# Mamba block with a Hadamard-rotated MLP: elementwise work moved from VectorE to GpSimd, inner channels split in PSUM, scan inputs made two groups ahead

## The chip, the cores and the metric

One Trainium2 chip; the program runs on one of its cores. The metric is the device time of one execution in microseconds, given as the median of three runs. The engines are called PE (TensorE; PEld is its weight load), DVE (VectorE), ACT (ScalarE), POOL (GpSimd) and SP (the queue that issues nearly all DMAs).

## The reference

The input is (4, 1024, 512) in float32, so 4096 tokens. `LN` has no gain and no bias.

```python
x = x + LN(mamba(LN(x)))
x = x + LN(ffn(LN(x)))

def mamba(h):                                   # 1024 inner channels, 16 states, conv of 4 taps
    hidden, gate = split(h @ W_in + b_in)
    u = silu(causal_depthwise_conv(hidden, conv_w, conv_b))
    dt, B, C = split(u @ W_x)                   # 128 + 16 + 16 columns
    delta = softplus(dt @ W_dt + b_dt)
    A = -exp(a_log)
    # over the tokens t, for each channel d and state n:
    #   h[d,n] = exp(delta[t,d] * A[d,n]) * h[d,n] + delta[t,d] * u[t,d] * B[t,n]
    #   y[t,d] = sum over n of h[d,n] * C[t,n]
    y = (y + u * d_param) * silu(gate)
    return y @ W_out + b_out

def ffn(z):                                     # 512 -> 2048 -> 512
    z = fwht(z * SU_ug) / 64                    # normalised Walsh-Hadamard transform
    a = silu(z @ W_gate.T * (ws_gate * 64)) * (z @ W_up.T * (ws_up * 64))
    a = fwht(a * SU_dp) / 64
    return a @ W_down.T * (ws_down * 64)
```

## The kernel before

The 4096 tokens go in 16 chunks `c` of 256 (`TC`), four chunks to a sequence. Channels lie on the partitions: `d` counts 8 blocks of 128 channels, `m` pairs of blocks, `g` groups of four states. A chunk has 8 x 4 = 32 scan groups, called slots, and everything else is hung on them: a plan (`STEADY`, and variants for the first, second and last chunk) says at which slot of which chunk each step is written down. While chunk `c` is scanned, the same 32 slots hold the out projection, both layernorms and the MLP's first half of chunk `c-1`, the MLP's second half of `c-2`, and the in projection, convolution, `x_proj`, delta and softplus of chunk `c+1`. This gives the order in which the program is written; the framework's planner then fixes the order on each engine from its own cost model. A queue works strictly in the order that it was given, and waits with all that stands behind.

One scan group (`scan`, L446) is: on DVE `h = du * b` (L461, 128x1024), where `du` is delta times u and sits in PSUM (L452, made once for a pair of blocks) and `b` is B spread over all partitions in SBUF; on ACT four exponentials into two PSUM buffers `da` (L469); on DVE two scans of 512 (L470), each of which waits for two of the exponentials; on POOL a copy of the last column to `state` (L472) and `h * c` (L473); where the plan's string `add` has a P, a POOL addition of the two halves of `h` (L478); and on PE 8 transposes of 128x128 (4 after an addition) that add up in the PSUM tile `yt` (L484). An exponential needs its `da` buffer back from the scan before last.

`h` has five buffers. The PSUM pool `mm` has four, one bank each, shared by all matmul outputs: `pp` (in projection), `pf` (MLP first half), `pq` (second half), `po` (out projection), `pd` (delta) and the transposes. The weight streams share five buffers (`ring`, L255).

The MLP's first half goes by 16 inner blocks `f`: 24 matmuls into `pf` (`inner`, L574), then `inner_act`: tanh on ACT (L588) and two DVE instructions (L589, L590) into `hf` in SBUF. `inner_parts` makes two float16 parts for a pair of blocks: ACT rounds `hf` to float16 (L595), POOL subtracts (L596). The matmuls of the second half (L608) take both parts.

`ln_stats` makes a layernorm's scale `rs` and offset `nm` for two 128-token tiles: DVE statistics (L200, L201), two to four tiny DVE instructions (L206 to L212), and a POOL power (L209). `add_normalised` adds the residual: ACT adds `nm` to x (L220), and DVE does `src * rs + x` (L221).

`softplus` (slots 30 and 31) is a chain ACT, DVE, ACT, DVE, POOL for the next chunk's delta, with a change of the activation table for the logarithm. `carry` takes the state over a chunk's border. `spread` loads one group's `b` and `c` (two DMAs of 512 KB on SP).

Of the kernel before, what the change touches and what calls it, by code (L numbers as in the profile page):

```python
# [114 lines left out]
def block_kernel(  # L115
# [77 lines left out]
    def ln_stats(src, name, scale=None):  # L193


        n = len(src)
        mv = sb.tile([P, NJ, 2], F32, tag="mv", name=f"mv_{name}", bufs=4)
        for i, t in enumerate(src):
            st = sb.tile([P, 6], F32, tag="st", name=f"st_{name}_{i}", bufs=4)
            nc.vector.bn_stats(st, t)  # L200
            nc.vector.bn_aggr(mv[:, i, :], st)  # L201
        rs = sb.tile([P, NJ], F32, tag="rs", name=f"rs_{name}", bufs=4)
        nm = sb.tile([P, NJ], F32, tag="nm", name=f"nm_{name}", bufs=4)
        v = rs[:, 0:n]
# [7 lines left out]
        nc.vector.scalar_tensor_tensor(nm[:, 0:n], mv[:, 0:n, 0], -1.0, v, ALU.mult, ALU.mult)  # L212
        return rs, nm
# [4 lines left out]
    def add_normalised(dst, src, rs, nm, j, x):  # L218

        nc.scalar.activation(x, x, AF.Identity, bias=nm[:, j : j + 1])  # L220
        nc.vector.scalar_tensor_tensor(dst, src, rs[:, j : j + 1], x, ALU.mult, ALU.add)  # L221

# [222 lines left out]

    def scan(c, d, g):  # L446
        first, last = c % NTC == 0, c % NTC == NTC - 1
        m, i = d // 2, d % 2
        dl = live["dl", c, d // 4][:, d % 4, :]
        if g == 0 and i == 0:  # L450
            du = ps_du.tile([P, 2, TC], F32, tag="du", name=f"du_{c}_{m}")
            nc.vector.tensor_tensor(  # L452
                du, live["dl", c, d // 4][:, d % 4 : d % 4 + 2, :], live["u", c, m], ALU.mult
            )
            live["du", c, m] = du
        ns = slice(g * GN, (g + 1) * GN)
        h = sb.tile([P, GN, TC], F32, tag="h", name=f"h_{c}_{d}_{g}", bufs=5)
# [3 lines left out]
        nc.vector.tensor_tensor(  # L461
            h[:, :, t:], live["du", c, m][:, i, t:].unsqueeze(1).to_broadcast([P, GN, TC - t]),
            live["b", c, g][:, :, t:], ALU.mult,
        )
# [6 lines left out]
        if not last:  # L471
            nc.gpsimd.tensor_copy(state[:, d, ns], h[:, :, TC - 1])  # L472
        nc.gpsimd.tensor_tensor(h, h, live["c", c, g], ALU.mult)  # L473
# [107 lines left out]
    def inner_act(c, f):  # L581

        if f == 0:
            live["hp", c] = fp.tile([P, NF, 2, TC], F16, tag="hp", name=f"hp_{c}", bufs=1)
        if f % 2 == 0:
            live["hf", c] = fp.tile([P, 2, TC], F32, tag="hf", name=f"hf_{c}_{f}", bufs=2)
# [3 lines left out]
        nc.vector.scalar_tensor_tensor(t, pp[:, 1, :], cf[:, f : f + 1], t, ALU.mult, ALU.mult)  # L590

    def inner_parts(c, f):
        hp, hf = live["hp", c], live.pop(("hf", c))
        at = slice(f - 1, f + 1)
        nc.scalar.copy(hp[:, at, 0, :], hf)  # L595
        nc.gpsimd.tensor_tensor(hp[:, at, 1, :], hf, hp[:, at, 0, :], ALU.subtract)  # L596

# [286 lines left out]
    for c in range(NCH):  # L884
# [215 lines left out]
```

## Time and profile before

| what | value |
|---|---|
| runs | 3088.71 us median (3088.61 to 3094.82) |
| the profiled execution | 3092.33 us, its span 3090.5 us |
| busy of the span | DVE 93%, PE 79%, POOL 68%, ACT 62%, PEld 60% |
| start, and first chunk | 0 to 51 us, 51 to 292 us |
| second chunk | 292 to 526 us |
| steady chunks from 884 to 2664 us (ten) | 178.0 us each |
| last chunk, and the end behind it | 2838 to 3026 us, 3026 to 3090 us |
| HBM read and written | 415.14 MB, 25.69 MB; DMA queue q1 43.1% |

A chunk is counted from its first scan. A group's row in the profile gives the line, engine, operation, tiles, shapes and count, then busy time and the mean length of one instruction, then the engine's idle time just before them and who ended it. Busy time is a union, so a group of overlapping instructions has less of it than count times mean.

### The profile page before, as it was taken

The numbers are of one execution on the slowest core, as the hardware profiler recorded it, in microseconds if no ns is written. First come the engines' busy times: TensorE is split into PE (matmuls) and PEld (weight loads), VectorE is DVE, ScalarE is ACT, GpSimd is POOL, SyncE is SP. The second block draws the span as 40 slices with busy tenths as digits, with TensorE's granted clock in tenths as the row PEclk, the third lists the DMA queues.
The fourth block names the chain that finished last, engine by engine and source line by source line (L and its number), as shares of the span: only waits on it lengthen the run. The fifth ranks groups of instructions, "written<-read, shape, count | busy, mean of one in ns | idle before, by whom it ended". The sixth has DMA issues, their size and how long they took to land.

```text
span 3090.5 us, 45909 instructions
## 1 busy us (share of the span) xinstructions
PE 2442.0 (79%) x16119; PEld 1846.4 (60%) x16119; DVE 2865.0 (93%) x3677; ACT 1924.5 (62%) x4321; POOL 2098.4 (68%) x1788
## 2 busy tenths in 40 slices
PE   4657578787897879788696978879777887868788
PEld 3446466574766657476574757566565756556556
DVE  7998998999999899999999999999999999899973
ACT  5657556576666757567575766667575666657542
POOL 2675666677776768667585877768676767768661
PEclk8778789899998989899898999989888999989999
DMA  5434246353353435334353534435343433535347
GB/s 209 177 103 144 72 126 199 110 158 135 117 184 124 151 123 166 102 127 168 109 185 116 166 121 136 159 110 171 132 155 117 151 136 110 177 102 173 122 153 249
DMA packets 154222, 443.82 MB, mean 144 GB/s; under 512 B 17928, under 2 KB 35208, under 8 KB 153992
## 3 DMA queue, kind: packets, MB, share of 16 engines
q1 hardware_dynamic: 153848, 440.83, 43.1%
q8 instruction: 127, 2.08, 0.3%
q14 instruction: 103, 0.84, 0.1%
q10 hardware_dynamic: 144, 0.07, 0.0%
HBM read 415.14 MB, written 25.69 MB: 143 GB/s over the span
## 4 chain that ended last, share of the span: by engine, by line
DVE 62%; PE 13%; issue 11%; POOL 7%; ACT 6%; DMA 1%; SPq 0%; DVEq 0%; POOLq 0%; ACTq 0%
DVE h L470 24%; DVE h L461 13%; DVE pp L313 4%; PE pf L574 4%; POOL h L473 3%; PE pq L608 3%; DVE du L452 2%; DVE hf L590 2%; PE pp L266 2%; PE yt L484 2%; DVE hf L589 2%; ACT da L469 1%; PE po L525 1%; DVE y L512 1%; POOL h L478 1%
## 5 line engine op out<-in xcount | busy, mean ns | idle before, releaser
L469 ACT ACTIVATE da<-dl,a_sb 128x255 f32<-128x255 f32 x2048 | 954.1, 474 | 765.3 <-DVE h L470 722.9
L473 POOL TENSOR_TENSOR h<-h,c 128x1024 f32<-128x1024 f32 x512 | 1228.1, 2402 | 175.5 <-DVE h L470 112.3
L470 DVE TENSOR_TENSOR_SCAN h<-da,h 128x512 f32<-128x512 f32 x1024 | 1216.2, 1205 | 25.2 <-ACT da L469 23.5
L574 PE MATMUL pf<-zT,wu 128*128 128x256 f16 x6144 | 756.8, 282 | 111.2 <-DVE hf L590 65.8
L574 PEld LDWEIGHTS <-wu 128*128 128x128 f16 x6144 | 620.0, 101 | 215.6 <-issue 118.6
L484 PE MATMUL yt<-ident,h 128*128 128x128 f32 x3180 | 476.5, 293 | 278.2 <-POOL h L473 96.3
L461 DVE TENSOR_TENSOR h<-du,b 128x1020 f32<-128x1020 f32 (+1 forms) x512 | 609.0, 1201 | 11.9 <-PE yt L484 11.0
L484 PEld LDWEIGHTS yt<-ident,h 128*128 128x128 f32 x3180 | 395.1, 151 | 352.1 <-POOL h L473 125.5
L472 POOL COPY state<-h 128x4 f32<-128x4 f32 x384 | 89.0, 232 | 512.9 <-DVE h L470 461.0
L608 PE MATMUL pq<-wd,hp 128*128 128x512 f16 x1536 | 368.3, 391 | 6.2 <-DVE o L543 4.3
L478 POOL TENSOR_TENSOR h<-h 128x512 f32<-128x512 f32 x226 | 300.2, 1329 | 4.6
L266 PE MATMUL pp<-xT,wh 128*128 128x256 f16 x1440 | 218.2, 322 | 56.2 <-DVE y L512 20.7
L608 PEld LDWEIGHTS <-hp 128*128 128x128 f16 x1536 | 154.4, 101 | 178.5 <-issue 32.0
L525 PE MATMUL po<-wo,y 128*128 128x512 f32 x512 | 231.4, 601 | 7.7 <-POOL y L515 5.2
L266 PEld LDWEIGHTS <-wh 128*128 128x128 f16 x1440 | 165.7, 116 | 105.4 <-issue 64.6
L266 PE MATMUL pp<-xT,wg 128*128 128x256 f16 x1536 | 189.9, 278 | 16.8 <-DVE zT L230 7.6
L596 POOL TENSOR_TENSOR hp<-hf,hp 128x512 f16<-128x512 f32 x128 | 158.5, 1239 | 62.6 <-ACT hp L595 62.2
L266 PEld LDWEIGHTS <-wg 128*128 128x128 f16 x1536 | 153.3, 100 | 49.2 <-issue 27.1
L313 DVE SCALAR_TENSOR_TENSOR pp<-pre,half,pp 128x256 f32<-128x256 f32 x384 | 179.0, 470 | 3.1 <-ACT pp L306 1.8
L588 ACT ACTIVATE hf<-pf,tf 128x256 f32<-128x256 f32 x256 | 119.5, 468 | 71.3 <-PE pf L574 70.9
L525 PEld LDWEIGHTS po<-wo,y 128*128 128x128 f32 x512 | 95.8, 193 | 113.3 <-issue 102.5
L589 DVE SCALAR_TENSOR_TENSOR hf<-hf,pf 128x256 f32<-128x256 f32 x256 | 103.1, 403 | 40.1 <-ACT hf L588 40.1
(195 smaller groups left out, 3039.6 us busy)
## 6 DMA issues: line engine op xcount, KB each, us to landing
wu<-ug SPq DMA_DIRECT2D x256, 512.0 KB, 3.4
wd<-dn SPq DMA_DIRECT2D x144, 512.0 KB, 3.6
b<-bcd SPq DMA_DIRECT2D x64, 512.0 KB, 4.1
c<-bcd SPq DMA_DIRECT2D x64, 512.0 KB, 5.4
wg<-win SPq DMA_DIRECT2D x64, 512.0 KB, 4.2
wo<-in_w_out_dram SPq DMA_DIRECT2D x64, 512.0 KB, 4.3
wh<-win SPq DMA_DIRECT2D x60, 512.0 KB, 3.9
x<-in_x_dram SPq DMA_DIRECT2D x32, 256.0 KB, 2.7
```

Source lines behind the costliest of these rows:

```text
L266: nc.tensor.matmul(pp[:, i, :], lhsT=wt[:, a, k, i * P : (i + 1) * P], rhs=xT[:, b, k, :], start=(n == 0), stop=(n == KD * len(PARTS) - 1),)
L313: nc.vector.scalar_tensor_tensor(pp[:, i, :], pre[:, i, k : k + TC], half[:, k * ND + d : k * ND + d + 1], pp[:, i, :], ALU.mult, ALU.add,)
L461: nc.vector.tensor_tensor(h[:, :, t:], live["du", c, m][:, i, t:].unsqueeze(1).to_broadcast([P, GN, TC - t]), live["b", c, g][:, :, t:], A ...
L469: exp = nc.scalar.activation(da[:, n, 1:], dl[:, 1:], AF.Exp, scale=a_sb[:, d, k : k + 1])
L470: add = nc.vector.tensor_tensor_scan(two, flat(da), two, 0.0, ALU.mult, ALU.add)
L473: nc.gpsimd.tensor_tensor(h, h, live["c", c, g], ALU.mult)
L478: (nc.gpsimd if by == "P" else nc.vector).tensor_tensor(h[:, 0:parts, :], h[:, 0:parts, :], h[:, parts:, :], ALU.add)
L484: nc.tensor.matmul(yt[:, j, :], lhsT=h[:, n, j * P : (j + 1) * P], rhs=ident, is_transpose=True, start=(g == 0 and n == 0 and j == 0), sto ...
L525: last = nc.tensor.matmul(live["po", c][j], lhsT=live["y", c, m][:, i, j * P : (j + 1) * P], rhs=wt[:, i, :], start=(m == 0 and i == 0), s ...
L574: nc.tensor.matmul(pp[:, w, :], lhsT=wt[:, w, k // 2, a, k % 2, :], rhs=zT[:, b, k, :], start=(n == 0), stop=(n == KD * len(PARTS) - 1),)
L589: nc.vector.scalar_tensor_tensor(t, t, 1.0, pp[:, 0, :], ALU.add, ALU.mult)
L608: nc.tensor.matmul(live["pq", c, j], lhsT=hp[:, 2 * q + i, b, j * P : (j + 1) * P], rhs=wt[:, :, i, a, :], start=(q == 0 and i == 0 and (a ...
```

## The change

GpSimd takes over `delta * u` (into SBUF, `dus`; ACT copies it to PSUM for the products that stay on DVE), ten of the 32 products `du * b` of a steady chunk (string `mul`; five in the second chunk, none in the first), the small layernorm instructions, and the residual sum, for which ACT now applies scale and offset in one instruction. In return ACT copies the `state` column, and the steady `add` string has ten P instead of sixteen. The inner channels' second DVE instruction writes into PSUM, ACT rounds from there to float16, PE subtracts the rounded part in PSUM with a matmul by -1, and ACT writes the rest as the second part, block by block. The input of a scan group is made two groups ahead (`prepare`, `AHEAD`), with seven `h` buffers. `x_proj`, delta and softplus come two to four slots earlier, `spread` two. The buffers of tag `pa`, which three setup steps used, are gone: these steps take `h` buffers.

```diff
+AHEAD = 2
 STEADY = dict(
-    x=(21, 23),
-    delta=(25, 26, 26, 27),
-    soft=(30, 31),
+    x=(19, 20),
+    delta=(22, 23, 23, 24),
+    soft=(27, 28),
-    add="-P---PP--PP--PP---P--PPP-PP-P-PP",
+    mul="--P--P--P--P--P--P--P--P--P--P--",
+    add="-P--P---P--P--P--P--P--P--P--P--",
 FIRST = STEADY | dict(
+    mul="-" * SLOTS,
-    delta=(23, 23, 24, 25),
-    soft=(30, 30),
+    x=(20, 21),
+    delta=(22, 23, 23, 24),
+    soft=(27, 28),
 SECOND = STEADY | dict(
+    mul="-----P-----P-----P-----P-----P--",
-    delta=(21, 26, 27, 28),
+    delta=(21, 22, 23, 24),
...
+    neg16 = cp.tile([P, P], F16, name="neg16")
+    nc.vector.tensor_scalar(neg16, ident, -1.0, None, ALU.mult)
...
         if scale is None:
-            nc.vector.tensor_scalar(v, mv[:, 0:n, 1], sc[:, INV_D2 : INV_D2 + 1], EPS, ALU.mult, ALU.add)
+            nc.gpsimd.tensor_scalar(v, mv[:, 0:n, 1], sc[:, INV_D2 : INV_D2 + 1], EPS, ALU.mult, ALU.add)
         else:
-            nc.vector.tensor_scalar(v, mv[:, 0:n, 1], EPS, scale ** -2, ALU.add, ALU.mult)
+            nc.gpsimd.tensor_scalar(v, mv[:, 0:n, 1], EPS, scale ** -2, ALU.add, ALU.mult)
         nc.gpsimd.tensor_tensor(v, v, mhalf[:, 0:n], ALU.pow)
         if scale is None:
-            nc.vector.tensor_scalar(v, v, sc[:, INV_D : INV_D + 1], None, ALU.mult)
-        nc.vector.scalar_tensor_tensor(nm[:, 0:n], mv[:, 0:n, 0], -1.0, v, ALU.mult, ALU.mult)
+            nc.gpsimd.tensor_tensor(v, v, sc[:, INV_D : INV_D + 1].to_broadcast([P, n]), ALU.mult)
+        nc.gpsimd.tensor_tensor(nm[:, 0:n], mv[:, 0:n, 0], v, ALU.mult)
+        nc.gpsimd.tensor_scalar(nm[:, 0:n], nm[:, 0:n], -1.0, 0.0, ALU.mult, ALU.add)
...
     def add_normalised(dst, src, rs, nm, j, x):
-        nc.scalar.activation(x, x, AF.Identity, bias=nm[:, j : j + 1])
-        nc.vector.scalar_tensor_tensor(dst, src, rs[:, j : j + 1], x, ALU.mult, ALU.add)
+        normalised(src, src, rs, nm, j)
+        nc.gpsimd.tensor_tensor(dst, src, x, ALU.add)
...
+    def inputs(c, m, eng=nc.gpsimd):
+        by = PLANS[c]["mul"][2 * NG * m : 2 * NG * (m + 1)]
+        dl = live["dl", c, m // 2][:, 2 * (m % 2) : 2 * (m % 2) + 2, :]
+        if "-" in by:
+            du = live["du", c, m] = ps_du.tile([P, 2, TC], F32, tag="du", name=f"du_{c}_{m}")
+        if c == 0:
+            nc.vector.tensor_tensor(du, dl, live["u", c, m], ALU.mult)
+            return
+        dus = live["dus", c, m] = sb.tile([P, 2, TC], F32, tag="dus", name=f"dus_{c}_{m}")
+        eng.tensor_tensor(dus, dl, live["u", c, m], ALU.mult)
+        if "-" in by:
+            nc.scalar.copy(du, dus)
+
+    def prepare(c, d, g):
+        first = c % NTC == 0
...
+        h = live["h", c, d, g] = sb.tile([P, GN, TC], F32, tag="h", name=f"h_{c}_{d}_{g}", bufs=7)
         t = 0 if first else 1
         if not first:
             nc.scalar.copy(h[:, :, 0], live["h_0", c, m][:, i, ns])
-        nc.vector.tensor_tensor(
-            h[:, :, t:], live["du", c, m][:, i, t:].unsqueeze(1).to_broadcast([P, GN, TC - t]),
+        pool = PLANS[c]["mul"][d * NG + g] == "P"
+        (nc.gpsimd if pool else nc.vector).tensor_tensor(
+            h[:, :, t:],
+            live["dus" if pool else "du", c, m][:, i, t:].unsqueeze(1).to_broadcast([P, GN, TC - t]),
             live["b", c, g][:, :, t:], ALU.mult,
         )
+
+    def scan(c, d, g):
...
         if not last:
-            nc.gpsimd.tensor_copy(state[:, d, ns], h[:, :, TC - 1])
+            nc.scalar.copy(state[:, d, ns], h[:, :, TC - 1])
...
     def inner_act(c, f):
-        pp, t = live.pop(("pf", c, f)), live["hf", c][:, f % 2, :]
+        pp, hp = live["pf", c, f], live["hp", c]
+        t = fp.tile([P, TC], F32, tag="hf", name=f"hf_{c}_{f}", bufs=3)
         nc.scalar.activation(t, pp[:, 0, :], AF.Tanh, scale=tf[:, f : f + 1])
         nc.vector.scalar_tensor_tensor(t, t, 1.0, pp[:, 0, :], ALU.add, ALU.mult)
-        nc.vector.scalar_tensor_tensor(t, pp[:, 1, :], cf[:, f : f + 1], t, ALU.mult, ALU.mult)
+        nc.vector.scalar_tensor_tensor(pp[:, 1, :], pp[:, 1, :], cf[:, f : f + 1], t, ALU.mult, ALU.mult)
+        nc.scalar.copy(hp[:, f, 0, :], pp[:, 1, :])
 
     def inner_parts(c, f):
-        hp, hf = live["hp", c], live.pop(("hf", c))
-        at = slice(f - 1, f + 1)
-        nc.scalar.copy(hp[:, at, 0, :], hf)
-        nc.gpsimd.tensor_tensor(hp[:, at, 1, :], hf, hp[:, at, 0, :], ALU.subtract)
+        pp, hp = live.pop(("pf", c, f)), live["hp", c]
+        nc.tensor.matmul(
+            pp[:, 1, :], lhsT=neg16, rhs=hp[:, f, 0, :], start=False, stop=True, skip_group_check=True
+        )
+        nc.scalar.copy(hp[:, f, 1, :], pp[:, 1, :])
...
-        t = pr.tile([P, 2 * D], F32, tag="pa", name=f"ntd_{i}")
+        t = sb.tile([P, 2 * D], F32, tag="h", name=f"ntd_{i}", bufs=7)
...
-        t = pr.tile([P, NF, DB], F32, tag="pa", name=f"da_{b}")
+        t = sb.tile([P, NF, DB], F32, tag="h", name=f"da_{b}", bufs=7)
         nc.sync.dma_start(t, w_down_t[b])
-        t1 = pr.tile([P, NF, DB], F32, tag="pa", name=f"db_{b}")
+        t1 = sb.tile([P, NF, DB], F32, tag="h", name=f"db_{b}", bufs=7)
...
-        if c % NTC != 0:
-            for m in range(1, NM):
-                at(c, 2 * NG * m - 5, carry, c, m)
+        for m in range(1, NM):
+            at(c, 2 * NG * m - 6, inputs, c, m)
+            if c % NTC != 0:
+                at(c, 2 * NG * m - 7, carry, c, m)
...
-            if b % NTC != 0:
-                at(c, SLOTS - 1, carry, b, 0)
+                if q == 0:
+                    at(c, when["soft"][0], inputs, b, 0)
+                    if b % NTC != 0:
+                        at(c, when["soft"][0], carry, b, 0)
             for g in range(NG):
-                at(c, SLOTS - NG + g, spread, b, g)
+                at(c, SLOTS - NG + g - AHEAD, spread, b, g)
...
     for s in range(NCH * SLOTS):
         if s == 2 * SLOTS:
             hold.close()
+        if s + AHEAD < NCH * SLOTS:
+            prepare((s + AHEAD) // SLOTS, (s + AHEAD) // NG % ND, (s + AHEAD) % NG)
         if s > 0:
             scan(s // SLOTS, s // NG % ND, s % NG)
```

More of the change, by code (lines that the diff above doesn't have):

```diff
@@ L444, in carry @@
         live["h_0", c, m] = h
-    def scan(c, d, g):
-        first, last = c % NTC == 0, c % NTC == NTC - 1
-        m, i = d // 2, d % 2
[L449 to L455, printed above, removed]
+    def inputs(c, m, eng=nc.gpsimd):
[12 more added lines that the diff above has]
+        first = c % NTC == 0
+        m, i = d // 2, d % 2
         ns = slice(g * GN, (g + 1) * GN)
-        h = sb.tile([P, GN, TC], F32, tag="h", name=f"h_{c}_{d}_{g}", bufs=5)
+        h = live["h", c, d, g] = sb.tile([P, GN, TC], F32, tag="h", name=f"h_{c}_{d}_{g}", bufs=7)
         t = 0 if first else 1
@@ L460, in scan @@
             nc.scalar.copy(h[:, :, 0], live["h_0", c, m][:, i, ns])
-        nc.vector.tensor_tensor(
-            h[:, :, t:], live["du", c, m][:, i, t:].unsqueeze(1).to_broadcast([P, GN, TC - t]),
+        pool = PLANS[c]["mul"][d * NG + g] == "P"
+        (nc.gpsimd if pool else nc.vector).tensor_tensor(
+            h[:, :, t:],
+            live["dus" if pool else "du", c, m][:, i, t:].unsqueeze(1).to_broadcast([P, GN, TC - t]),
             live["b", c, g][:, :, t:], ALU.mult,
         )
+    def scan(c, d, g):
+        last = c % NTC == NTC - 1
+        dl = live["dl", c, d // 4][:, d % 4, :]
+        ns = slice(g * GN, (g + 1) * GN)
+        h = live.pop(("h", c, d, g))
         for q in range(2):
@@ L584, in inner_act @@
             live["hp", c] = fp.tile([P, NF, 2, TC], F16, tag="hp", name=f"hp_{c}", bufs=1)
-        if f % 2 == 0:
-            live["hf", c] = fp.tile([P, 2, TC], F32, tag="hf", name=f"hf_{c}_{f}", bufs=2)
-        pp, t = live.pop(("pf", c, f)), live["hf", c][:, f % 2, :]
+        pp, hp = live["pf", c, f], live["hp", c]
+        t = fp.tile([P, TC], F32, tag="hf", name=f"hf_{c}_{f}", bufs=3)
         nc.scalar.activation(t, pp[:, 0, :], AF.Tanh, scale=tf[:, f : f + 1])
         nc.vector.scalar_tensor_tensor(t, t, 1.0, pp[:, 0, :], ALU.add, ALU.mult)
-        nc.vector.scalar_tensor_tensor(t, pp[:, 1, :], cf[:, f : f + 1], t, ALU.mult, ALU.mult)
+        nc.vector.scalar_tensor_tensor(pp[:, 1, :], pp[:, 1, :], cf[:, f : f + 1], t, ALU.mult, ALU.mult)
+        nc.scalar.copy(hp[:, f, 0, :], pp[:, 1, :])
     def inner_parts(c, f):
-        hp, hf = live["hp", c], live.pop(("hf", c))
-        at = slice(f - 1, f + 1)
-        nc.scalar.copy(hp[:, at, 0, :], hf)
-        nc.gpsimd.tensor_tensor(hp[:, at, 1, :], hf, hp[:, at, 0, :], ALU.subtract)
+        pp, hp = live.pop(("pf", c, f)), live["hp", c]
[3 more added lines that the diff above has]
+        nc.scalar.copy(hp[:, f, 1, :], pp[:, 1, :])
     def down(c, q, js=range(NJ)):
@@ L632, in block_kernel @@
     h_sb = pr.tile([P, P], F32, name="h_sb", bufs=1)
-    wf = [sb.tile([P, KD, 2 * P], F32, tag="h", name=f"wf_{m}", bufs=5) for m in range(NM)]
-    wf += [pr.tile([P, KD, 2 * P], F32, tag="pa", name=f"wf_{m}") for m in range(NM, 2 * NM - 1)]
+    wf = [sb.tile([P, KD, 2 * P], F32, tag="h", name=f"wf_{m}", bufs=7) for m in range(NM)]
+    wf += [sb.tile([P, KD, 2 * P], F32, tag="h", name=f"wf_{m}", bufs=7) for m in range(NM, 2 * NM - 1)]
     wf += [sb.tile([P, KD, 2 * P], F32, tag="ring", name=f"wf_{2 * NM - 1}", bufs=5)]
@@ L720, in block_kernel @@
         softplus(0, 0, 1, nc.vector)
+        inputs(0, 0)
+        for s in range(AHEAD):
+            prepare(0, 0, s)
         for ins in scan(0, 0, 0):
@@ L949, in block_kernel @@
                 at(c, i + 1, inner_act, b, f)
-                if f % 2 == 1:
-                    at(c, i + 1, inner_parts, b, f)
+                at(c, i + 1, inner_parts, b, f)
         if c > 1:
@@ L1025, in block_kernel @@
             inner_act(c, f - 1)
-            if f % 2 == 0:
-                inner_parts(c, f - 1)
+            inner_parts(c, f - 1)
     inner_act(c, NF - 1)
```

## The prediction

> **What bounds the kernel now.** I read the engine shares first, then the stretches between chunk borders (a chunk runs from its first scan to the next one's), then the groups of the ten steady chunks alone, then the waits. The first lines are the page's, the next the stretches: length, busy time of PE, PEld, DVE, ACT, POOL, the granted PE clock, DMA share, GB/s.
>
> ```profile
> span 3090.5 us, 45909 instructions
> PE 2442.0 (79%) x16119; PEld 1846.4 (60%) x16119; DVE 2865.0 (93%) x3677; ACT 1924.5 (62%) x4321; POOL 2098.4 (68%) x1788
> ```
>
> ```profile
> 292.00:526.00 234.00, 172.02 (x1064) 131.61 (x1063) 214.89 (x299) 136.05 (x305) 151.45 (x134) 0.85 0.41 128
> ...
> 884.00:2664.00 1780.00, 1450.52 (x9817) 1096.39 (x9816) 1700.56 (x2130) 1152.88 (x2608) 1278.55 (x1101) 0.91 0.42 140
> ...
> 3026.00:3090.00 64.00, 56.53 (x422) 40.99 (x419) 18.83 (x43) 13.03 (x24) 10.34 (x10) 0.98 0.66 227
> ```
>
> The middle line is ten steady chunks of 178.0 us. In each, DVE is busy 170.1 us and idle 7.9, PE 145.1 busy and 32.9 idle, POOL 127.9, ACT 115.3. DVE bounds it; the next engine is PE at 81%. The groups of that stretch, with the instructions that go, and those that show what they will cost elsewhere:
>
> ```profile
> L473 POOL TENSOR_TENSOR h<-h,c 128x1024 f32<-128x1024 f32 x320 | 766.2, 2398 | 96.5 <-DVE h L470 66.3 <-PE po L525 5.0 <-DVE nm_d L212 4.3
> L484 PE MATMUL yt<-ident,h 128*128 128x128 f32 x1920 | 285.2, 290 | 158.5 <-issue 49.8 <-POOL h L478 46.7 <-POOL h L473 46.3
> L461 DVE TENSOR_TENSOR h<-du,b 128x1020 f32<-128x1020 f32 x228 | 271.3, 1200 | 6.5 <-PE yt L484 6.1 <-POOL h L473 0.3
> L478 POOL TENSOR_TENSOR h<-h 128x512 f32<-128x512 f32 x160 | 212.1, 1327 | 3.3
> L596 POOL TENSOR_TENSOR hp<-hf,hp 128x512 f16<-128x512 f32 x81 | 100.7, 1243 | 17.3 <-ACT hp L595 17.0
> L452 DVE TENSOR_TENSOR du<-dl,u 128x512 f32<-128x512 f32 x40 | 56.6, 1414 | 16.0 <-POOL dl L421 15.9
> L472 POOL COPY state<-h 128x4 f32<-128x4 f32 x256 | 56.1, 219 | 316.0 <-DVE h L470 287.5 <-PE po L525 6.5 <-DVE nm_d L212 4.6
> L515 POOL TENSOR_TENSOR y<-y,g 128x512 f32<-128x512 f32 x40 | 50.9, 1273 | 12.9 <-DVE y L512 12.9
> L595 ACT CAST hp<-hf 128x512 f16<-128x512 f32 x81 | 49.7, 614 | 19.8 <-DVE hf L590 19.8
> L420 DVE SCALAR_TENSOR_TENSOR dl<-dl,sp_w 128x1024 f32<-128x1024 f32 x20 | 36.9, 1844 | 2.9 <-ACT sp_w L419 2.9
> L221 DVE SCALAR_TENSOR_TENSOR x<-o,rs_b,xr 128x512 f32<-128x512 f32 x20 | 28.9, 1472 | 0.0
> L221 DVE SCALAR_TENSOR_TENSOR e<-e,rs_d,x 128x512 f32<-128x512 f32 x20 | 25.9, 1328 | 2.1 <-ACT x L220 2.1
> ```
>
> The waits of the same stretch say who follows whom:
>
> ```profile
> ACT da L469 <- DVE h L470: 438.3, 358, 6.0
> POOL state L472 <- DVE h L470: 287.5, 153, 9.2
> ...
> PE pf L574 <- DVE hf L590: 43.9, 27, 4.9
> ```
>
> ACT and POOL stand still for DVE's scans; PE waits for POOL's products (the L484 row), so for DVE at second hand, and for PSUM buffers that DVE gives back. Little waits the other way.
>
> **The change, per steady chunk.**
>
> *DVE.* Ten products: a product adds about 1.06 us to DVE's busy time (319 in the stretch add 338.7 us to the union; mean length 1.20), so 10.6. du: 56.6 / 10 = 5.7. Residual: (28.9 + 25.9) / 10 = 5.5. Tiny layernorm instructions L206, L208, L211, L212: 3.4 + 16.8 + 10.3 + 24.3 = 54.8 / 10 = 5.5. Sum 27.3, DVE falls to 142.8.
>
> *The rule against it.* By the rows, one 128x1024 product costs 1.20 us on DVE and 2.40 on POOL (L473), and the Trainium skill says the same and draws the opposite conclusion: "GPSIMD Engine Reference", section Engine selection, wants elementwise work on VectorE, being about twice as fast. Counted as work, ten moved products cost 24.0 us for 10.6; counted by the engine that is full, they gain 10.6, since POOL has 50.1 us idle and DVE 7.9. The page's Key points add that GpSimd shares SBUF interfaces with VectorE, which clashes with VectorE instructions that have two SBUF inputs. Here rows split: L221, du and L420 have two and run at 1.33 to 1.84 us, while products and scans (one input in PSUM) keep to 1.2 us. If a fuller POOL slowed every DVE instruction, the gain would go; by the rows it can slow only what still has two, the four softplus instructions (the least L420 took is near 1.2 for this size), so I add 1 us. DVE: 144.
>
> *POOL.* Ten products 24.0; du 4 x 1.27 (L515, same size) = 5.1; residual sums 5.1; 13 tiny instructions, not seen on POOL in this form: between the state copy's 0.22 and the power's 0.70 (L209), I take 0.25, near the tiny additions of the carry (0.24 to 0.28), 3.3 (at most 9.1). Less six additions of 1.33 (8.0), L596 (10.1), L472 (5.6). POOL: 127.9 + 13.8 = 141.7.
>
> *PE.* Six additions fewer mean 24 more transposes at 285.2 / 1920 = 0.149: 3.6 (up to 7 unpipelined at 0.29). The 16 matmuls by -1: 0.125 pipelined (an L574 matmul) to 0.39 alone with its weight load; I take 0.2: 3.2. PE: 152. The granted clock rose with PE's load in the shown stretches (0.85, 0.91, 0.98), so this may shrink by some per cent; I don't count on it.
>
> *ACT.* 32 copies of 256 out of PSUM at 0.37 (L498) = 11.8; 24 state copies at 0.18 = 4.3; four du copies at 0.61 = 2.4; fuller residual +0.4; less L595, 5.0. ACT: 129. Two waits are new. The state copy waits for a group's second scan; if it stands before the next exponentials, each is late by up to one scan, 1.1 us, up to 27 us a chunk; I take 0, as the planner can put it behind them, and exponentials wait for that same engine anyway. And the matmul by -1 waits for ACT's copy, with PE's next work queued behind it, while its `pf` bank is held through two ACT copies and a place in PE's queue: 0 to some 5 us each. Covers are the 24 matmuls (about 3 us) of the next block and three other `mm` banks; I price it within PE's idle below.
>
> *What moves.* The border: in the softplus chain near 1580 us DVE had 6 of the chunk's 7.9 us of idle. With softplus three slots earlier and inputs two ahead, scans can go on over it; late next would be DVE's scan behind the logarithm's two table loads (1.28 us each) on ACT. I keep 7.9 us as DVE's loss. The eight `spread` DMAs (b lands in a median 4.1, c in 5.4 us) pass two slots of SP's queue: b's buffer is free earlier, c's isn't, so a c load may stop the queue for two slots, with weight streams behind. Five ring buffers cover it (PE's weight loads waited for `wu` DMAs 7.4 us in the whole run), so 0; without cover a late load is 4 us. `x_split`'s small DMAs and the delta matmuls move with slack on both sides.
>
> *Sum.* DVE alone would allow 144 + 7.9 = 152 us. But then PE (152) would be full, and it does not run full anywhere: its densest long stretch is the end, 56.5 of 64 us (88%). At 92% (its clock higher, waits for DVE gone) 152 us of work make 165; DVE is then 87%, POOL 86%, ACT 78% busy. So 178 to 165, times 14 chunks (thirteen steady ones and the last): -182. Second chunk: five products, du, residual and layernorm off DVE, about -20, of which I give back 10, since `dn_load` takes `h` buffers two at a time from the scan. First chunk: its wf and norm tiles also take `h` buffers, +8. End: 16 matmuls by -1 and longer chains in the MLP, +3. Together 3090.5 - 182 - 10 + 8 + 3 = 2909.5 of span, 1.8 outside it (3092.33 less 3090.5) and 3.6 by which the profiled execution is over the median: 2908. About 0.2%, 6 us, is what a measurement can tell from no change.
>
> **The rivals.**
>
> *DVE stays the bound and runs full* (152 a chunk): 14 x 26 = 364 less, about 2725. For it: PE's and POOL's idle is mostly DVE's doing. Against: three engines within 10 us of each other and one in-order queue each. Chance 0.10.
>
> *ACT becomes the brake.* An exponential pair takes 0.95 us in a scan's 1.13; without products between the scans, any copy in between delays a scan. For it: 60 more small ACT instructions a chunk. Against: only 18.6 us of DVE waiting for `da` in ten chunks now, and 36 us a chunk of ACT idle left. About 10 us of new DVE waits: 172 to 175 a chunk, 2990 to 3080. Chance 0.12, and 0.04 for within 0.2%.
>
> *PE's idle is not slack: slower.* PE needs 152 us, and if none of its 32.9 us idle is recovered, because it stops at the matmuls by -1, for `mm` banks held longer, and for `h` behind a busier POOL, a chunk takes 185: 14 x 6.7 = 94 more, 3180. It decides from the point where PE recovers less than 6.6 us of its idle. For it: PE already waits for banks (`pf` for L590). Against: those waits end with a DVE that is late today. Chance 0.22.
>
> The likeliest case (2840 to 2980) has 0.52. **The numbers:** faster 0.10 + 0.52 + 0.12 = 0.74, same 0.04, slower 0.22. From 2780 to 3150 about a tenth is left out at each end.
>
> **What would show it.** Right: steady chunks of 160 to 170 us, DVE 140 to 146 us busy in each, POOL near 142, PE 148 to 155; no long stop of the scans at borders. L420 near 1.9 us if only two-input instructions suffer. Wrong: products L461 or scans above 1.25 us (contention everywhere); DVE waiting for `da` by over 5 us a chunk (the ACT rival); PE idle of 30 us a chunk with its waits at the matmul by -1 or for `mm` banks (the PE rival); tiny POOL instructions of 0.7 us; the first two chunks longer than 241 and 234 us.

## The result, and the profile after

The changed kernel takes 3160.42 us (median of four runs, 3158.28 to 3163.49), the kernel before 3090.53 us in the runs beside it: a ratio of 1.0225, 95% interval 1.0207 to 1.0243. It is slower by 70 us, where 181 us less were forecast. The page after:

```profile
span 3161.5 us, 47011 instructions
...
PE 2475.9 (78%) x16711; PEld 1917.8 (61%) x16711; DVE 2532.5 (80%) x3258; ACT 2106.2 (67%) x5149; POOL 2265.3 (72%) x1679
```

DVE fell from 93% to 80%, as it was meant to, and no engine took its place: nothing is over 80%. The stretches after, from first scans (ten steady chunks; the last chunk; the end), same columns as before:

```profile
902.00:2704.00 1802.00, 1471.14 (x10213) 1144.21 (x10214) 1478.73 (x1863) 1268.71 (x3147) 1393.78 (x1014) 0.90 0.40 138
...
2878.00:3066.00 188.00, 147.12 (x967) 108.21 (x966) 129.42 (x157) 103.93 (x255) 128.98 (x84) 0.87 0.34 117
3066.00:3162.00 96.00, 85.26 (x588) 57.74 (x586) 26.63 (x56) 25.39 (x58) 16.19 (x37) 0.98 0.68 242
```

| stretch | before | after | after less before |
|---|---|---|---|
| start, to the first scan | 51.2 | 51.4 | +0.2 |
| first chunk | 240.6 | 232.7 | -7.9 |
| second chunk | 234.4 | 236.4 | +2.0 |
| thirteen chunks after it | 2311.9 | 2357.2 | +45.3 |
| last chunk and end | 252.4 | 283.8 | +31.4 |

A steady chunk takes 180.2 us, before 178.0. The groups of the steady chunks that answer to those shown of before:

```profile
L497 POOL TENSOR_TENSOR h<-h,c 128x1024 f32<-128x1024 f32 x320 | 758.1, 2379 | 274.8 <-ACT state L496 223.5 <-DVE h L494 39.3 <-ACT da L493 10.8
...
L508 PE MATMUL yt<-ident,h 128*128 128x128 f32 x2160 | 316.9, 300 | 164.2 <-POOL h L502 111.1 <-ACT ys L522 45.3 <-POOL h L497 7.8
...
L478 DVE TENSOR_TENSOR h<-du,b 128x1020 f32<-128x1020 f32 x159 | 190.0, 1206 | 12.6 <-PE yt L508 6.6 <-ACT du L466 5.0
L478 POOL TENSOR_TENSOR h<-dus,b 128x1020 f32<-128x1020 f32 x72 | 169.7, 2358 | 9.0 <-PE yt L508 8.7
...
L426 DVE SCALAR_TENSOR_TENSOR sp_e<-sp_w,sp_e 128x1024 f32<-128x1024 f32 x20 | 53.1, 2654 | 8.8 <-ACT sp_w L425 8.8
...
L619 PE MATMUL pf<-hp,neg 128*128 128x256 f16 x161 | 43.7, 278 | 30.1 <-ACT hp L614 30.1
...
L428 DVE SCALAR_TENSOR_TENSOR dl<-dl,sp_w 128x1024 f32<-128x1024 f32 x20 | 26.3, 1317 | 10.8 <-ACT sp_w L427 10.8
...
L216 POOL TENSOR_TENSOR rs_c<-rs_c,mhalf 128x2 f32<-128x2 f32 x10 | 7.0, 702 | 0.1
...
L219 POOL TENSOR_TENSOR nm_c<-mv_c,rs_c 128x2 f32<-128x2 f32 x10 | 2.0, 196 | 0.2
```

The durations are near those forecast: 1.21 us for a product on DVE, 2.36 on POOL, 0.20 for a tiny instruction (forecast 1.20, 2.40, 0.25). The waits of the same stretch:

```profile
ACT da L493 <- DVE h L494: 249.0, 213, 5.1
POOL h L497 <- ACT state L496: 223.5, 68, 9.7
PE yt L508 <- POOL h L502: 111.1, 21, 10.4
DVE pp L321 <- ACT pp L314: 71.2, 25, 4.9
PE pt_c L235 <- ACT xm L224: 61.0, 10, 9.5
```

The last line is the one to follow: once a chunk PE stands 6 us at the transposes of `xm`, the layernorm ahead of the MLP. Before it stood 2.2 us there:

```profile
PE pt_c L227 <- ACT xm L216: 22.1, 10, 4.2
```

One chunk cut in three (the tenth, from its first scan) shows what a chunk's mean hides. Before:

```profile
1776.00:1835.00 59.00, 44.34 (x236) 25.86 (x234) 56.69 (x67) 34.87 (x80) 43.89 (x42) 0.94 0.38 125
1835.00:1880.00 45.00, 36.23 (x283) 30.67 (x282) 45.00 (x71) 29.53 (x71) 27.39 (x28) 0.85 0.39 129
1880.00:1953.00 73.00, 64.16 (x466) 51.93 (x465) 69.46 (x81) 52.57 (x122) 59.80 (x56) 0.98 0.50 164
```

And after:

```profile
1809.00:1868.00 59.00, 54.32 (x302) 33.73 (x300) 54.07 (x64) 41.53 (x108) 49.50 (x36) 0.94 0.41 137
1868.00:1913.00 45.00, 24.01 (x138) 19.05 (x137) 35.77 (x42) 27.48 (x73) 44.59 (x35) 0.70 0.13 43
1913.00:1987.00 74.00, 67.68 (x590) 61.10 (x588) 57.71 (x83) 58.93 (x151) 46.12 (x38) 1.00 0.58 200
```

In the middle 45 us POOL is busy 44.6 and PE 24.0; in the 74 us behind PE is busy 67.7 and POOL 46.1. The two take turns. The chunk is no exception: in the same 45 us of all ten chunks PE is busy 22.9 us and POOL 44.3 in the mean, before 34.8 and 26.3. PE's idle time in the stretch shown is 8.5 us for `xm`, 8.4 for POOL's sums of `h` (L502) and 4.1 for ACT's `ys`. What `xm` waits for stands in POOL's timeline of that stretch (start, length, what):

```profile
1873.55 0.19 POOL L215 TENSOR_SCALAR rs_c<-mv_c 128x2 f32<-128x2 f32 x1
1873.82 1.26 POOL L502 TENSOR_TENSOR h<-h 128x512 f32<-128x512 f32 x1
1875.04 1.26 POOL L539 TENSOR_TENSOR y<-y,g 128x512 f32<-128x512 f32 x1
1876.27 2.35 POOL L497 TENSOR_TENSOR h<-h,c 128x1024 f32<-128x1024 f32 x1
...
1878.80 2.34 POOL L478 TENSOR_TENSOR h<-dus,b 128x1020 f32<-128x1020 f32 x1
1881.10 0.69 POOL L216 TENSOR_TENSOR rs_c<-rs_c,mhalf 128x2 f32<-128x2 f32 x1
1881.76 2.34 POOL L497 TENSOR_TENSOR h<-h,c 128x1024 f32<-128x1024 f32 x1
...
1888.23 2.35 POOL L478 TENSOR_TENSOR h<-dus,b 128x1020 f32<-128x1020 f32 x1
1890.54 0.20 POOL L219 TENSOR_TENSOR nm_c<-mv_c,rs_c 128x2 f32<-128x2 f32 x1
1890.69 2.35 POOL L497 TENSOR_TENSOR h<-h,c 128x1024 f32<-128x1024 f32 x1
...
1899.06 0.19 POOL L220 TENSOR_SCALAR nm_c<-nm_c 128x2 f32<-128x2 f32 x1
```

Four tiny instructions of 1.3 us in all form one layernorm's scale and offset. They begin at 1873.6 and end at 1899.3, because POOL's queue is full and long instructions stand between one and the next: here eleven, of which two are moved products (L478) and the others work that POOL had before, `h * c` (L497) most of all. `xm`, `zT` and the 384 matmuls of the MLP's first half wait for the last of them.

For the experiments I take three numbers from each trace as means over the same ten chunks (fifth to fourteenth): the **c chain**, from the end of the second `mv_c` (L201 before, L208 after) to the end of the last `nm_c`; the **long instructions**, those of POOL over 1 us that run within it; and **o to zT**, from the start of the first addition of the out projection to the end of the last `zT` on DVE. Before: 9.3 us, 3.3 and 51.2 us. After: 29.5 us, 13.5 and 68.0 us. They leave out that the first addition itself starts 33.0 us into a chunk after the change, before at 19.0; the fastest kernel below has 28.7, so this start alone is not the loss.

### The profile page after: what moved, and what is told of

The parts are those of the page before. It is cut to its first block, busy times and chain, and to the rows that moved or that the text cites. A ratio compares the mean times of both kernels' runs of the same rounds, so it can differ in the third digit from the quotient of the medians.

```text
span 3161.5 us, 47011 instructions
## 1 busy us (share of the span) xinstructions
PE 2475.9 (78%) x16711; PEld 1917.8 (61%) x16711; DVE 2532.5 (80%) x3258; ACT 2106.2 (67%) x5149; POOL 2265.3 (72%) x1679
## 4 chain that ended last, share of the span: by engine, by line
DVE 39%; PE 26%; ACT 18%; POOL 7%; issue 7%; DMA 2%; SPq 0%; DVEq 0%; POOLq 0%; ACTq 0%
DVE h L494 19%; PE pf L598 9%; DVE h L478 6%; ACT da L493 5%; PE pp L274 4%; PE po L549 4%; POOL h L497 4%; PE pq L634 3%; DVE pp L321 2%; PE yt L508 2%; DVE sp_e L426 2%; POOL h L478 1%; DVE pf L613 1%; ACT pre L308 1%; ACT g L344 1%
## 5 line engine op out<-in xcount | busy, mean ns | idle before, releaser
L497 POOL TENSOR_TENSOR h<-h,c 128x1024 f32<-128x1024 f32 x512 | 1214.2, 2380 | 489.1 <-ACT state L496 381.6
L508 PE MATMUL yt<-ident,h 128*128 128x128 f32 x3516 | 518.1, 301 | 259.9 <-POOL h L502 166.1
L508 PEld LDWEIGHTS yt<-ident,h 128*128 128x128 f32 x3516 | 455.9, 156 | 332.6 <-POOL h L502 177.3
L478 DVE TENSOR_TENSOR h<-du,b 128x1020 f32<-128x1020 f32 (+1 forms) x367 | 438.8, 1207 | 47.5 <-PE yt L508 29.6
L478 POOL TENSOR_TENSOR h<-dus,b 128x1020 f32<-128x1020 f32 (+1 forms) x145 | 343.7, 2372 | 14.6 <-PE yt L508 13.9
L634 PE MATMUL pq<-wd,hp 128*128 128x512 f16 x1536 | 343.0, 379 | 3.0 <-DVE o L567 1.6
L549 PE MATMUL po<-wo,y 128*128 128x512 f32 x512 | 244.0, 621 | 1.6 <-ACT hp L622 1.6
L274 PE MATMUL pp<-xT,wh 128*128 128x256 f16 x1440 | 194.3, 298 | 16.0 <-DVE g L346 6.4
L502 POOL TENSOR_TENSOR h<-h 128x512 f32<-128x512 f32 x142 | 182.1, 1283 | 2.1
L539 POOL TENSOR_TENSOR y<-y,g 128x512 f32<-128x512 f32 x64 | 93.6, 1463 | 102.9 <-DVE y L536 102.8
```

What stands on the lines that cost most here:

```text
L274: nc.tensor.matmul(pp[:, i, :], lhsT=wt[:, a, k, i * P : (i + 1) * P], rhs=xT[:, b, k, :], start=(n == 0), stop=(n == KD * len(PARTS) - 1),)
L478: (nc.gpsimd if pool else nc.vector).tensor_tensor(h[:, :, t:], live["dus" if pool else "du", c, m][:, i, t:].unsqueeze(1).to_broadcast([P ...
L502: (nc.gpsimd if by == "P" else nc.vector).tensor_tensor(h[:, 0:parts, :], h[:, 0:parts, :], h[:, parts:, :], ALU.add)
L508: nc.tensor.matmul(yt[:, j, :], lhsT=h[:, n, j * P : (j + 1) * P], rhs=ident, is_transpose=True, start=(g == 0 and n == 0 and j == 0), sto ...
L549: last = nc.tensor.matmul(live["po", c][j], lhsT=live["y", c, m][:, i, j * P : (j + 1) * P], rhs=wt[:, i, :], start=(m == 0 and i == 0), s ...
L634: nc.tensor.matmul(live["pq", c, j], lhsT=hp[:, 2 * q + i, b, j * P : (j + 1) * P], rhs=wt[:, :, i, a, :], start=(q == 0 and i == 0 and (a ...
```

## The experiments

Theory L: the layernorm's tiny instructions are late in POOL's queue because of the products there, the MLP's input comes late, PE idles and then is full. Rivals: M, POOL has too much work; I, the inner channels' split holds PE; S, the state copy on ACT holds POOL's `h * c`.

### One part undone at a time

**x_lnres**: layernorm instructions and residual sums back on DVE.

```diff
-            nc.gpsimd.tensor_scalar(v, mv[:, 0:n, 1], EPS, scale ** -2, ALU.add, ALU.mult)
+            nc.vector.tensor_scalar(v, mv[:, 0:n, 1], EPS, scale ** -2, ALU.add, ALU.mult)
...
-        nc.gpsimd.tensor_tensor(nm[:, 0:n], mv[:, 0:n, 0], v, ALU.mult)
-        nc.gpsimd.tensor_scalar(nm[:, 0:n], nm[:, 0:n], -1.0, 0.0, ALU.mult, ALU.add)
+        nc.vector.scalar_tensor_tensor(nm[:, 0:n], mv[:, 0:n, 0], -1.0, v, ALU.mult, ALU.mult)
...
-        normalised(src, src, rs, nm, j)
-        nc.gpsimd.tensor_tensor(dst, src, x, ALU.add)
+        nc.scalar.activation(x, x, AF.Identity, bias=nm[:, j : j + 1])
+        nc.vector.scalar_tensor_tensor(dst, src, rs[:, j : j + 1], x, ALU.mult, ALU.add)
```

> The changed kernel with the tiny layernorm instructions and the residual sums back on DVE as before; all else as changed. Theory L (the layernorm chain stands between 2.4 us products in POOL's queue, so the MLP's input zT comes late: out projection added at 33 us of a chunk and zT ready at 101, 68 us, where before it took 51; PE then idles in mid chunk and is full at its end): that stretch falls to about 50 us, PE's waits for xm (6 us a chunk) go, a steady chunk takes 165 to 172 us, the whole 2930 to 3040 us. Theory M (POOL is simply overfull in the first half of a chunk with products), I (inner split) and S (state copy on ACT): within 1% of the changed kernel's 3160 us, since only 8 us of POOL work a chunk go and 11 us come back to DVE.

**x_mul**: no product on POOL.

```diff
-    mul="--P--P--P--P--P--P--P--P--P--P--",
+    mul="-" * SLOTS,
...
-    mul="-----P-----P-----P-----P-----P--",
+    mul="-" * SLOTS,
```

> The changed kernel with no product du*b on POOL (all 32 of a chunk on DVE); du is still made by POOL and copied by ACT, all else as changed. Theory M: POOL loses 24 us a chunk, its full stretch (95 to 99% in the first half of a chunk) goes, the whole falls by over 120 us to 3040 or less. Theory L: shorter queues before the layernorm instructions help as well, but DVE gets 10.6 us a chunk back: 3080 to 3140 us. Theories I and S: within 1% of 3160.

**x_inner**: `inner_act` and `inner_parts` as before.

```diff
-        nc.scalar.copy(hp[:, f, 0, :], pp[:, 1, :])
...
-        nc.tensor.matmul(
-            pp[:, 1, :], lhsT=neg16, rhs=hp[:, f, 0, :], start=False, stop=True, skip_group_check=True
-        )
-        nc.scalar.copy(hp[:, f, 1, :], pp[:, 1, :])
+        nc.scalar.copy(hp[:, at, 0, :], hf)
+        nc.gpsimd.tensor_tensor(hp[:, at, 1, :], hf, hp[:, at, 0, :], ALU.subtract)
```

> The changed kernel with the inner channels split as before (ACT rounds a pair of blocks, POOL subtracts, no matmul by -1); all else as changed. Theory I (the in-order PE stops at the matmuls by -1, mm banks are held longer, ACT has 16 us more of copies a chunk): PE's waits for ACT hp (about 9 us a chunk) go and the whole falls by 80 us or more to 3080 or less. Theory L and M: POOL gets 10 us a chunk more in the second half of the chunk, where it is half idle: within 1% of 3160.

**x_state**: the state copy back on POOL.

```diff
-            nc.scalar.copy(state[:, d, ns], h[:, :, TC - 1])
+            nc.gpsimd.tensor_copy(state[:, d, ns], h[:, :, TC - 1])
```

> The changed kernel with the state copy on POOL as before; all else as changed. Theory S (POOL's h*c, which overwrites h in place, now has to wait for ACT's state copy: 22 us a chunk of POOL waits carry its name): the whole falls by 60 us or more to 3100 or less. Theory L and M: that wait is the wait for the scan at second hand (the copy starts 0.03 us after the scan in the median), and POOL gets 5 us more a chunk: 3150 to 3190 us.

| kernel | us, median | ratio to before, interval | c chain | long | o to zT |
|---|---|---|---|---|---|
| x_lnres | 2980.04 | 0.9648 (0.9633 to 0.9664) | 7.0 | 3.2 | 45.4 |
| x_mul | 3019.13 | 0.9771 (0.9756 to 0.9785) | 8.6 | 3.8 | 49.6 |
| x_inner | 3150.62 | 1.0198 (1.0183 to 1.0213) | 33.6 | 15.8 | 79.8 |
| x_state | 3217.26 | 1.0416 (1.0399 to 1.0433) | 25.8 | 10.8 | 72.7 |

S falls: the state copy back on POOL costs 57 us (27 more than L and M allowed), and POOL then waits for the scan at the copy itself, 360 us in the whole run, where it waited 382 us at `h * c` for ACT's copy. That wait was the wait for the scan at second hand. Undoing the inner split gives 10 us, not the 80 of I. But this run alone does not clear the split: `zT` is ready later (111 us into a chunk, in the changed kernel 101), and the 384 matmuls behind it then take 75 us from first to last in place of 88, so that two effects nearly cancel. What speaks against I are the kernels below that keep the split and are faster than before. L and M were each right once: x_lnres fell into L's range where M forecast no change, and x_mul into M's (3040 or less) where L forecast 3080 to 3140. Either part taken back makes the kernel 141 to 180 us faster than the changed one and faster than before, which speaks for the two together.

### Layernorm alone, products alone, products elsewhere

**x_ln** takes the tiny layernorm instructions alone back to DVE (the first two pieces of x_lnres's diff). **x_mul_late** keeps ten products a chunk on POOL but puts them all in its second half:

```diff
-    mul="--P--P--P--P--P--P--P--P--P--P--",
+    mul="------------------PP-PP-PP-PP-PP",
```

**x_lnres_mul** is x_lnres and x_mul together, and **b_lnres** the kernel before with the changed `ln_stats` and `add_normalised` and nothing else.

> The changed kernel with only the tiny layernorm instructions back on DVE (the residual sums stay on POOL). Theory L, that each tiny instruction stands behind a product of 2.4 us and four of them make the chain: it gives most of what both together gave (3160 to 2980), so 2970 to 3040. If the residual sums, two of 1.3 us in the same queue, were the late link, it stays above 3090.

> The changed kernel with its ten products of a steady chunk all in slots 18 to 31, where POOL was 40 to 74% busy, none in slots 0 to 17, where the layernorms run and POOL was 87 to 99% busy; the amount of work on each engine is the same. Theory L: the stretch from the out projection's addition to zT shrinks from 68 to about 50 us, the whole to 3000 to 3090. Theory M in the form that the amount of work on POOL counts, wherever it stands: 3140 to 3180.

> The changed kernel with layernorm instructions and residual sums back on DVE and no product on POOL either. Tells whether the ten products gain anything once the layernorm is out of POOL's queue. If they relieve the engine that bounds: DVE gets 10.6 us a chunk back, so 3040 to 3130, slower than 2980. If they only filled POOL's queue (theory M): 2900 to 2960.

> The kernel before with only the tiny layernorm instructions and the residual sums moved to POOL. DVE loses 11 us a chunk, which alone would make it 150 us faster. Theory L: the chain from the out projection's addition to zT grows from 51 us by some 10 to 20 and takes back all or more: 3080 to 3200. If the chain hurts only together with the products on POOL: 2950 to 3050.

| kernel | us, median | ratio to before, interval | c chain | long | o to zT |
|---|---|---|---|---|---|
| x_ln | 2965.32 | 0.9600 (0.9581 to 0.9619) | 11.0 | 6.9 | 48.0 |
| x_mul_late | 3011.87 | 0.9745 (0.9729 to 0.9761) | 11.4 | 6.3 | 49.5 |
| x_lnres_mul | 3091.00 | 1.0004 (0.9995 to 1.0013) | 5.4 | 1.7 | 43.7 |
| b_lnres | 2980.96 | 0.9647 (0.9633 to 0.9662) | 13.6 | 6.2 | 56.3 |

M falls as a matter of amount: x_mul_late gives POOL the same work (138.8 us a chunk, in the changed kernel 139.4) in another place, and is 149 us faster. My expectation that b_lnres would lose falls too: the layernorm on POOL is good (110 us) as long as no products stand in the same queue. With x_lnres, x_mul and x_lnres_mul this makes a square. With neither: 3091; layernorm and residual on POOL: 3019, 72 less; products on POOL: 2980, 111 less. If they added up, both would give 3091 - 72 - 111 = 2908. Both give 3160.

### Which layernorm

There are four a chunk. `c` is ahead of the MLP, `b` ahead of it at the residual; `a` (a later chunk's in projection) and `d` (the output) are not on the way to `zT`. **x_lnc**, **x_lnad** and **x_lnbc** take only those named back to DVE:

```diff
+        if name[0] in "c":
+            nc.vector.tensor_scalar(v, mv[:, 0:n, 1], EPS, scale ** -2, ALU.add, ALU.mult)
+            nc.gpsimd.tensor_tensor(v, v, mhalf[:, 0:n], ALU.pow)
+            nc.vector.scalar_tensor_tensor(nm[:, 0:n], mv[:, 0:n, 0], -1.0, v, ALU.mult, ALU.mult)
...
```

> The changed kernel with the tiny instructions of one layernorm alone back on DVE: that ahead of the MLP (names with c), two DVE instructions in place of three on POOL, once a chunk; the other three layernorms and the residual sums stay on POOL. Theory L in its narrow form, that the late link is the scale for zT (29.5 us from mv_c to nm_c, before 9.3): most of the gain of moving all four, so 2960 to 3040. If all the small instructions together fill POOL's queue, a fifth or so of it: 3110 to 3160.

> The control to that: the tiny instructions of the two layernorms that the MLP's input does not wait for (a, ahead of the in projection of a later chunk, and d, at the MLP's output) back on DVE, b and c stay on POOL. It takes more small instructions off POOL (7 a chunk) than the other. Theory L, narrow: 3110 to 3180. If POOL's count of small instructions is what matters: under 3080.

> The changed kernel with the tiny instructions of the two layernorms on the way to zT (b and c) on DVE, and a and d on POOL. Theory L: about as fast as all four on DVE, 2940 to 3000. If a and d on POOL cost as much: above 3030.

| kernel | us, median | ratio to before, interval | c chain | long | o to zT |
|---|---|---|---|---|---|
| x_lnc | 3011.47 | 0.9738 (0.9723 to 0.9754) | 13.7 | 7.1 | 56.2 |
| x_lnad | 3270.74 | 1.0581 (1.0564 to 1.0599) | 31.7 | 15.6 | 78.7 |
| x_lnbc | 2936.64 | 0.9504 (0.9484 to 0.9524) | 12.7 | 7.0 | 48.3 |

Three instructions a chunk off POOL, 0.6 us of its work, make the kernel 149 us faster (x_lnc). Seven others make it 110 us slower. That was not expected: in x_lnad's order of instructions the chain of b is longer too (18.1 us, in the changed kernel 12.5), and `zT` is ready 11 us later; why that order came about has no run of its own. x_ln and x_lnbc came out 5 and 3 us below their ranges. The c layernorm carries most of it, b the rest of what can be had, and a and d do better on POOL. x_lnbc, 5% faster than before, is the fastest of all. Its ten chunks from 861 to 2507 us take 164.6 us each (forecast: 165). A stretch of nearly those chunks, and PE's wait for `xm` in the ten:

```profile
865.00:2600.00 1735.00, 1508.13 (x10652) 1160.48 (x10651) 1595.25 (x2001) 1309.04 (x3301) 1461.35 (x1006) 0.94 0.45 149
...
PE pt_c L245 <- ACT xm L234: 82.4, 10, 13.5
```

DVE is 92% busy, PE 87%, POOL 84%, ACT 75%. PE stands at `xm` for 8.2 us a chunk, longer than in the changed kernel, and the kernel is the fastest: that wait shows where the chain ends, and its length does not measure the loss.

### Order or amount

Was it the place in the queue? **x_prio**, **x_prio_c** and **x_prio_res** raise the planner's priority for all tiny instructions, for those of c, and for the residual sums too:

```diff
+        with tc.high_priority():
             nc.gpsimd.tensor_scalar(v, mv[:, 0:n, 1], EPS, scale ** -2, ALU.add, ALU.mult)
```

> The changed kernel, every instruction on its engine as changed; only the planner is told to take the tiny layernorm instructions on POOL ahead of all others that are ready. Theory L as a matter of order: the stretch from mv_c to nm_c falls from 29.5 to under 12 us, few long instructions stand inside it, the whole falls to 2900 to 2990. If POOL's amount of work is the cause: 3120 to 3180.

> The same for the one layernorm ahead of the MLP alone. Theory L, narrow: the same stretch falls to under 12 us, the whole to 2950 to 3030 (its tiny instructions on DVE gave 3011). If amount is the cause: 3120 to 3180.

> As for all layernorms, and the two residual sums of each are taken ahead as well. If the chain to zT still sets the pace of a chunk: 10 to 40 us faster than without them. If it no longer does: within 0.5% of that kernel.

They took 3154.76, 3155.02 and 3156.70 us (ratios 1.0213, 1.0210, 1.0219), and say nothing: in their traces all 1679 POOL instructions stand in the same order as in the changed kernel, and those of DVE, ACT and PE too. I suppose that priority chooses among instructions that are ready, and that each tiny one becomes ready only when the one before it is done, by when the planner has put a long one in the gap; no run shows the planner's choice itself. If so, steps count, not instructions. **x_hop3** makes the same four tiny instructions with the negation first, off the chain: three in a row in place of four. **x_hop3_late** adds x_mul_late's string.

```diff
+        nc.gpsimd.tensor_scalar(nm[:, 0:n], mv[:, 0:n, 0], -1.0, 0.0, ALU.mult, ALU.add)
...
-        nc.gpsimd.tensor_tensor(nm[:, 0:n], mv[:, 0:n, 0], v, ALU.mult)
-        nc.gpsimd.tensor_scalar(nm[:, 0:n], nm[:, 0:n], -1.0, 0.0, ALU.mult, ALU.add)
+        nc.gpsimd.tensor_tensor(nm[:, 0:n], nm[:, 0:n], v, ALU.mult)
```

> The changed kernel with the mean's negation ahead of the chain: three dependent tiny instructions on POOL in place of four, the same number in all, the same engines. If each step of the chain waits for the long instructions that the planner puts between (13.5 over the c chain, some three or four a step): the stretch from mv_c to nm_c falls from 29.5 us to 18 to 24, the whole to 3040 to 3130. If POOL's amount of work is the cause: 3140 to 3180.

> The changed kernel with the negation out of the chain and the ten products in slots 18 to 31. Against the same products with four steps (3012): 2970 to 3005 if the chain still sets the pace there, 3005 to 3030 if not.

x_hop3: 3085.55 us, ratio 0.9985 (0.9978 to 0.9992), c chain 20.9 us with 10.3 long instructions. x_hop3_late: 3006.71 us, 0.9723 (0.9706 to 0.9740), chain 11.0. One dependent step less, with every instruction on the same engine, takes 8.6 us off the chain and 75 us off the kernel. With the products out of the way already it gives 5 us, no more than the same order of instructions differed between two rounds of runs (3160 and 3155).

One caution goes with the other experiments, x_hop3 too: the planner made a new order on all engines for each, so a run shows an edit together with its order. What holds across the orders is that a late `zT` goes with a long chunk: it is ready 86 us into a chunk of 172.1 in x_lnc, 94 of 175.2 in x_hop3, 101 of 180.2 in the changed kernel, 106 of 185.4 in x_state, 112 of 189.4 in x_lnad. x_inner, with the other split, stands apart (111 of 181.1), and where `zT` comes at 70 to 81 us, chunks take 164.6 to 177.8 us in no such order: there something else sets the pace.

### Other combinations

**x_ln_late** is x_ln with x_mul_late's string, **x_ln_inner** x_ln with the inner split of before.

> All tiny layernorm instructions on DVE and the ten products in slots 18 to 31. If placing products away from POOL's full stretch adds to the layernorm's cure: 2900 to 2955. If the cure is all there is to have, and late products now meet softplus and the border: 2960 to 3020.

> All tiny layernorm instructions on DVE, and the inner channels split as before (POOL subtracts, no matmul by -1). With the layernorm cured PE is 84% busy; if the matmuls by -1 and the two extra ACT copies a block hold it, 2900 to 2950; if POOL is now nearer to the bound (10 us a chunk more there), 2975 to 3020.

2998.94 us (0.9702, 0.9688 to 0.9717) and 2996.23 us (0.9689, 0.9674 to 0.9705), both behind x_ln's 2965. With the layernorm cured, spread products are 34 us better than late ones, and the changed inner split gains 31 us.

## Why the prediction was wrong

**Engine work was right within 5 us a chunk.** Per steady chunk: DVE 147.9 us (1478.73 / 10; forecast 144), PE 147.1 (152), POOL 139.4 (141.7), ACT 126.9 (129). Tiny layernorm instructions without the power cost POOL 2.6 us (forecast 3.3).

**The step that failed** is "13 tiny instructions ... 3.3": priced as POOL's work, with no question of what stands ahead of each in POOL's queue and who waits for the last. As work they were 2.6 us. As a chain, c's alone went from 9.3 to 29.5 us, and o to zT from 51 to 68, with PE's next 384 matmuls behind. The change put a chain of four steps and ten more products of 2.4 us into one queue, worked in its fixed order, and the sum treated the two as independent. What it forecast, 2908, is what the square gives if they add; that the two agree to the microsecond is chance.

**The step after it** failed with it: 152 us of PE work "at 92%" is a mean over a chunk. In the stretch of 45 us shown above PE ran 24.0 us with POOL full, then 67.7 of 74 with POOL 62% busy. Neither was a bound by its mean (82 and 77%), each was one for a part of it. With b and c back on DVE the 165 us a chunk are there (164.6), so the loss is not in the other moves. But there DVE is 92% busy and PE 87%, where the forecast had 87 and 92: that the size is met is luck in part.

**The slower rival** was near in time (3180 against 3160) and right that PE's idle was not recovered: 147.1 us of work leave 33 us idle, as before. Its causes were not: PE waits for `hp` at the matmul by -1 only 3.0 us a chunk, and for banks held until ACT's second copy (L622) 4.7 us, where it waited 7.1 us before for those that L590 gave back; undoing the split gave 10 us. (Its own sum should have read 6.9 us a chunk, 152 + 32.9 less 178.0, in place of 6.7.) "`h` behind a busier POOL" was the nearest it came. The ACT rival: DVE waits for `da` 32.2 us in ten chunks, not 100. It does wait for ACT elsewhere (convolution 71.2, MLP 64.7, gate 47.3 us), but that goes with the late layernorm: with b and c on DVE these three are 13.0, 15.1 and 18.0 us, in x_lnbc's ten chunks.

**The rule of the Trainium skill** ("GPSIMD Engine Reference", Engine selection and Key points). The clash that its Key points name came where they say. Products and scans kept to 1.21 us beside a fuller POOL; of the DVE groups over 0.2 us that both kernels have, only those with two SBUF inputs moved by more than 4%. L426 after was L418 before:

```profile
L418 DVE SCALAR_TENSOR_TENSOR sp_e<-sp_w,sp_e 128x1024 f32<-128x1024 f32 x21 | 35.4, 1687 | 8.1 <-ACT sp_w L417 8.1
```

It went from 1.69 to 2.65 us, while L420, now L428, fell from 1.84 to 1.32. The four cost 0.7 us a chunk more (53.1 + 26.3 against 35.4 + 36.9, per ten); 1 us was forecast. Advice to keep elementwise work off GpSimd would have been right for the changed kernel as it stands, but not for the page's reason: ten products there gain 111 us where no layernorm chain shares the queue.

**The border**: scans still stop there (20.2 us from the last group's first scan to the next chunk's, averaged over ten chunks, in x_ln, 20.1 before, 22.6 after). Earlier softplus bought nothing, since what it waits for came later: the next chunk's last `u` is done 53.4 us ahead of the border before and 44.5 after.

**First and second chunk**: forecast +8 and -10, measured -8 and +2. **Last chunk and end**: forecast -10, measured +31; in x_lnbc +8 (260.3 us), so with b and c undone most of it goes, and the remaining 8 us have no run of their own.

## What to carry to other kernels

A tiny instruction moved to an engine with room is not priced by its length: count the dependent steps of its chain, put ahead of each what the queue holds between two of them (here some three long instructions a step, 13.5 over four), and ask who waits for the last. Before two moves to one engine are added up, look whether they meet in the same stretch; here each alone gained 72 or 111 us, and both lost 69. If a chain must share a queue with long work, take steps out of it or put the long work elsewhere in time: one step was worth 75 us, another place of the products 149, each with the order that the planner made of it.

## What the hardware showed beyond that

The granted PE clock moved within one chunk: 0.70 in the stretch where PE was starved, 1.00 in the next, 0.94 in the one ahead (before: 0.94, 0.85, 0.98). In the starved stretch it stood at 0.50 from 1884.8 to 1908.7 us, 5.5 us beyond the end of the wait for `xm`: the first 24 `pp` matmuls behind that wait took 4.63 us, and 23 of the same shape, at 1.00 a little later, 2.67. So part of a starved stretch is paid again in slower matmuls.

POOL's `y * g`, the same 512 elements, took 1273 ns before and 1495 in the changed kernel, in the mean of forty. Thirty-one of them took 1.26 to 1.30 us and nine 2.25 to 2.27, and each of the nine began while L426 ran, the DVE instruction with two SBUF inputs. Of such a pair the one that begins later is the one that becomes longer. L426 begun beside a running `h * c` took up to 3.25 us; in x_inner it begins first in sixteen of twenty cases, takes 1.20 to 1.23 us, and the `h * c` beside it takes 3.04 to 3.37 in place of 2.4. So the length of L426 goes by what it meets, and not by POOL's load: 1.64 us in the mean of x_inner, with POOL 82% busy, and 2.65 in the changed kernel, with 77%.
